# Layer 0's experts: two loads of weights wait also for the last store of layer 1's projected values

## The chip, the cores and the metric

The kernel runs on one core of one Trainium2 chip. The metric is the device time of one launch in microseconds; a kernel's time is the median of its runs. All data are 32-bit floats.

## The reference, cut to what matters

Four layers work on `x` (2 x 512 tokens of width 256). Each layer is a cross-attention against a context `ctx_1024` (2 x 1024 rows of width 256), followed by a feed-forward part with eight experts. The change lies in layer 0's experts, where work for layer 1's attention is done as well. Cut from the reference:

```python
x = x + _L0_xattn_ref(_layernorm(x), ctx_1024, ...)
x = x + _L0_ffn_ref(_layernorm(x), L0_ffn_router_w, L0_ffn_router_b, L0_ffn_w1, L0_ffn_w2)
x = x + _L1_xattn_ref(ctx_1024, _layernorm(x), ...)     # and so on to layer 3

def _L0_ffn_ref(...):            # 1024 tokens, 8 experts, hidden width 1024
    route = softmax(x @ router_w + router_b)
    max_prob, max_ind = max(route), argmax(route)
    for e in range(8):
        a, g = split(x @ w1[e], 2)
        y = silu(a) * g @ w2[e]
        out = where(max_ind == e, y, out)
    return out * max_prob

def _L1_xattn_ref(x, latents, ...):   # x is the context here
    xn = layer_norm(x, gamma_x, beta_x)
    kv_x = xn @ Wkv                   # keys and values: 512 columns each
    ...
```

Layer 1's keys and values of the context (`kv_x`) don't depend on layer 0, so the kernel can project them ahead of time.

## The kernel before

Layer 0's expert part begins with the router (normalise `X`, transpose, logits, softmax, the best expert of each token). `slots_of` gives each token a row ("slot") in the scratch tensor `xd` in DRAM. `moe` then does this, in the order of the code:

1. Eight indirect DMAs on POOL (L429) scatter the normalised tokens into `xd`; the list `put` holds them.
2. `filler()`, here `first_batch`: the context is transposed into `cT`, and `ahead1` projects layer 1's keys and values for the first of the two batches. These are sixteen jobs (eight of keys, eight of values): two `mm2` products into a PSUM tile `pk` (tags `a` and `g` in turn, two buffers each), a copy on ACT (ScalarE) into an SBUF tile of tag `sk` (two buffers; `sk` at L644 for keys, `sv` at L664 for values), and a store of 256 KB on ACT's queue to `kd` (L648) or `vd` (L665).
3. The experts' tiles. Expert weights are rows of `L0_experts`; one expert's tile `w` is 128 x 6144 floats (3072 KB), from a pool with four buffers. There are four pair tiles (`pair_tile`), which serve two experts with 64 slots each and so load two `w` (L475, on SP's queue), and six to eleven overflow tiles (`slot_tile`) of 128 slots for one expert, whose weights are gathered by an indirect DMA on POOL (L536). The loop runs pair 0, slot tile 4, pair 1, slot tile 5, and so on. Ahead of pairs 1 to 3 `between` puts two of the second batch's key jobs (`ahead1`).

Each tile loads its 128 slots from `xd` (`xs`, L455, on SP), transposes them on TensorE (PE, L464), copies them to `sT` on VectorE (L466) and runs the products. In a pair tile these are `half` (L489, into `pa` of tag `a` and `pg` of tag `g`, the same PSUM buffers that `pk` uses), the transposes `turn` (L503) and `product` (L510). In a slot tile they are `mm2` (L132) into `pa` and `pg`, and the second product (L561). The result goes to `yd` by ACT's queue.

The four `w` buffers go, in this order, to pair 0 (two), slot tile 4 and pair 1's first load; pair 1's second load takes a buffer of pair 0 when that is done, slot tile 5's load takes the other one, and so on. Pair 0's two loads are issued during the end of layer 0's attention (468.34 us).

`behind_slots(x)` makes a DMA `x` wait on a semaphore for the landing of `first_slots[0]`, the first tile's `xs` load. It is called for both loads of pairs 1 to 3, and for the slot tile 4's load (`if front < E and s == front`).

The order of instructions on each engine and queue is made by the framework from dependencies and readiness, not taken over from the code: on SP, the `xs` loads of four tiles stand ahead of pair 1's first weight load, though the code has them in turn. Each queue runs its instructions in order; one that waits holds up those behind it. The code pins an order only where it says so (`keep_in_program_order`, `pe_in_order`), which this stage does not. A `tc.If` after the last certain tile holds the rare overflow tiles, and after it comes the gather of the results (`combine`), on which layer 1 depends.

Of the kernel before, what the change touches and what calls it, by code (L numbers as in the profile page):

```python
# [33 lines left out]
def tile_kernel(ctx: ExitStack, tc: tile.TileContext, d: dict, out: bass.AP):  # L34
    nc = tc.nc
# [12 lines left out]
    def load_rows(pool, src, tag, bufs=None):  # L48

        rows, cols = src.shape  # L50
        return load(pool, [P, rows // P, cols], src.rearrange("(t p) f -> p t f", p=P), tag, bufs)

    def load_bc(pool, src, tag):

        n = src.shape[0]
        return load(pool, [P, n], src.partition_broadcast(P), tag)
# [48 lines left out]
    def to_T(*args, **kw):  # L105
        for _ in turn_blocks(*args, **kw):
            pass
# [21 lines left out]
    def mm2(ps_ap, lhsT, lcols, rhs, rcols):  # L129

        for dc in range(2):
            nc.tensor.matmul(  # L132
                ps_ap, lhsT[:, dc, lcols], rhs[:, dc, rcols], start=(dc == 0), stop=(dc == 1)
            )
# [110 lines left out]
    def bc8(a):  # L245
        return a[:, :, None].to_broadcast([P, TT, E])
# [4 lines left out]
    def router_logits(ps, srcT, w):  # L251
        pl = ps.tile([P, TT, E], F32, tag="mm", name="pl")
        for t in range(TT):
            mm2(pl[:, t, :], srcT, slice(t * P, (t + 1) * P), w, slice(0, E))
        lg = rt("lg")
        nc.vector.tensor_copy(lg, pl)
        return lg

    def maxed(src, name):
        m = rt(name, (TT,))  # L260
        nc.vector.tensor_reduce(m, src, AX.X, ALU.max)
        return m

    def summed(src, name):
        m = rt(name, (TT,))
        nc.vector.tensor_reduce(m, src, AX.X, ALU.add)
        return m
# [141 lines left out]
    def moe(L, ps, hp, ep, rows, slots, wrow, used, F, act, glu, finish, filler=None, hold=None, between=None):  # L409
# [13 lines left out]
        for i, si in enumerate(slots):  # L423
            if named and i == 0:
                nc.vector.tensor_copy(rows[:, :, D], c_tok)
            for t in range(TT):
                if i == 1:
                    nc.vector.tensor_scalar(rows[:, t, D:], c_tok[:, t : t + 1], float(NT), None, ALU.add)
                x = nc.gpsimd.indirect_dma_start(  # L429
                    out=xd, out_offset=bass.IndirectOffsetOnAxis(ap=si[:, t : t + 1], axis=0), in_=rows[:, t, :], in_offset=None  # L430
                ).ins
                for y in put:
                    tc.declare_no_dep(x, y, reason="rows of different slots")
                put.append(x)
        if filler is not None:
            filler()
        wd = d[f"{L}_experts"]
        WC = wd.shape[1]

        first_slots = []  # L440

        def behind_slots(x):

            tc.add_manual_dep(
                x, first_slots[0].name, mybir.DependencyInfo(mybir.DependencyClass.Sync, mybir.DependencyReason.DATA),
                reason="not among the transfers that the first tile waits for",
            )

        def parts(w):
            w1 = w[:, 0 : 2 * W1].rearrange("p (c f) -> p c f", c=2)  # L450
# [183 lines left out]
    def ahead(ps, st, L, w, src, jobs, values, bias=None, n_bias=1):  # L634


        for i, job in enumerate(jobs):
            pk = ps.tile([P, 512], F32, tag="ag"[i % 2], name="pk")
            if job[0] == "k":
                _, row, col, cols, c0 = job  # L640
                mm2(pk, w, cols, src, slice(c0, c0 + 512))
                k = st.tile([P, 512], F32, tag="sk", name="sk", bufs=2)
                if bias is None:
                    nc.scalar.copy(k, pk)  # L644
                else:
                    j = row // P % n_bias
                    nc.scalar.activation(k, pk, AF.Identity, bias=bias[:, j : j + 1])
                nc.scalar.dma_start(kds[L][row : row + P, col : col + 512], k)  # L648
            else:
                values(pk, job[1])  # L650

    kds, vds = {}, {}

    def ahead1(ps, st, w, cT, b, part=slice(None)):

        if b == 0:
            kds["L1"] = dram.tile([B * 4 * P, S], F32, tag="L1kd", name="kd")
            vds["L1"] = dram.tile([B * S, 512], F32, tag="L1vd", name="vd")

        def values(pv, kt):  # L660
            r = slice(b * S + kt * P, b * S + (kt + 1) * P)
            mm2(pv, cT, r, w, slice(512, 1024))
            v = st.tile([P, 512], F32, tag="sk", name="sv", bufs=2)
            nc.scalar.copy(v, pv)  # L664
            nc.scalar.dma_start(vds["L1"][r, :], v)  # L665

        jobs = []
        for pr in range(4):
            for hf in range(2):
                jobs.append(("k", (b * 4 + pr) * P, hf * 512, slice(pr * P, (pr + 1) * P), b * S + hf * 512))  # L670
        jobs += [("v", kt) for kt in range(8)]
        ahead(ps, st, "L1", w, cT, jobs[part], values)

    def ahead16(ps, st, L, params, nkt):

        one17, wk, wv, bk, bv = params[1:4] + params[5:7]
        NK = nkt * P
        kds[L] = dram.tile([B * 4 * P, NK], F32, tag=f"{L}kd", name="kd")
        vds[L] = dram.tile([B * NK, 512], F32, tag=f"{L}vd", name="vd")
        vs = [st.tile([P, 2, 16, 32], F32, tag=f"sv{i}", name="sv", bufs=1) for i in range(2)]  # L680
        for v in vs:
            nc.gpsimd.memset(v, 1.0)

        def values(pv, n):
            b, k2 = divmod(n, nkt // 2)
            v = vs[n % 2]
            for i in range(2):
                c0 = b * S + (k2 * 2 + i) * P
                mm2(pv[:, i * D : (i + 1) * D], cTr, slice(c0, c0 + P), wv, slice(0, D))
            from_ps = pv.rearrange("p (i h c) -> p i h c", i=2, c=16)  # L690
            if bv is None:
                nc.scalar.copy(v[:, :, :, 0:16], from_ps)
            else:
                for i in range(2):
                    nc.vector.tensor_add(v[:, i, :, 0:16], from_ps[:, i], bv.rearrange("p (h c) -> p h c", c=16))
            r0 = b * NK + k2 * 2 * P
            nc.scalar.dma_start(
                vds[L][r0 : r0 + 2 * P, :].rearrange("(i p) f -> p i f", p=P), v.rearrange("p i h c -> p i (h c)")
            )

        jobs = []
        for b in range(B):
            for g in range(4):
                for hf in range(NK // 512):
                    jobs.append(("k", (b * 4 + g) * P, hf * 512, slice(g * P, (g + 1) * P), b * S + hf * 512))
        jobs += [("v", n) for n in range(B * nkt // 2)]
        bias, cols = (one17, 1) if bk is None else (bk, 4)
        ahead(ps, st, L, wk, cTr, jobs, values, bias, cols)
# [51 lines left out]
    def psum(tags, name):  # L760

        return tc.tile_pool(name=name, bufs=tags, space=PSUM, reuse_waits="tile")

    def normed(pool, twice, tag="xn", width=D):
        xn = pool.tile([P, TT, width], F32, tag=tag, name="xn")
        layernorm(xn[:, :, 0:D], X, TT, twice)
        return xn
# [3 lines left out]
    with (  # L771
# [39 lines left out]
        cT = cp.tile([P, 2, B * S], F32, tag="cT", name="cT")  # L811
# [215 lines left out]
    wkv = load_rows(pp, d["L1_xattn_Wkv"], "wkv")  # L1027
# [4 lines left out]
    with (  # L1032
        tc.tile_pool(name="L0f", bufs=1, reuse_waits="tile") as fp,
        tc.tile_pool(name="L0h", bufs=2, reuse_waits="tile") as hp,
        tc.tile_pool(name="L0g", bufs=4, reuse_waits="tile") as ep,
        psum(2, "L0fps") as ps,
    ):
        rw = load_rows(fp, d["L0_ffn_router_w"], "rw")
        rb = load_bc(fp, d["L0_ffn_router_b"], "rb")
        xT = fp.tile([P, 2, B * S], F32, tag="cT", name="xT")  # L1040
        xn = normed(fp, False)
        to_T(ps, xT, xn, TT)
        lg = router_logits(ps, xT, rw)
        nc.vector.tensor_add(lg, lg, rb[:, None, :].to_broadcast([P, TT, E]))
        nc.vector.tensor_sub(lg, lg, bc8(maxed(lg, "m1")))
        nc.scalar.activation(lg, lg, AF.Exp)
        tot = summed(lg, "m2")
        nc.vector.reciprocal(tot, tot)
        nc.vector.tensor_mul(lg, lg, bc8(tot))
        mp = maxed(lg, "m1")  # L1050
        oh = first_of(lg, mp, "oh1")
        slots, wrow, used = slots_of(ps, [oh], 11, 64)
        cT = fp.tile([P, 2, B * S], F32, tag="cT", name="cT")

        def first_batch():
            to_T(ps, cT, C, CT, g_c, b_c, "g")
            ahead1(ps, hp, wkv, cT, 0)

        def between(s):

            if s > 0:
                ahead1(ps, hp, wkv, cT, 1, slice(2 * s - 2, 2 * s))

        yd = moe("L0", ps, hp, ep, xn, slots, wrow, used, 1024, AF.Silu, True, plain, first_batch, None, between)
        ahead1(ps, hp, wkv, cT, 1, slice(6, None))
        combine(fp.tile([P, TT, D], F32, tag="xn", name="yg"), yd, slots, [mp], X)

# [521 lines left out]
    first = {}  # L1589
# [268 lines left out]
```

## Time and profile before

| | before |
|---|---|
| time, median of 3 runs (lowest to highest) | 2259.86 us (2259.75 to 2261.13) |
| the profiled execution's own time | 2264.73 us |
| span of its trace | 2262.7 us |
| mean granted clock of PE | 0.95 |
| PE busy | 2070.5 us (92%) |
| VectorE (DVE), ACT, POOL busy | 1083.6, 859.6, 439.3 us |
| layer 0's experts: first weights issued, first pair product, gather of results | 468.34, 529.03, 667.18 us |

A profiled execution is about 5 us longer than the median here, of which 2 us lie around the span. Times inside the trace count from the start of the span. In rows of the trace, `pa<-w,sT` reads "the tile `pa` is written from `w` and `sT`", `x8` counts records, and a float32 product of two matrices shows as two records. A bracket at the end of a timeline row gives the idle time of the engine ahead of it and what ended that.

### The profile page before, as it was taken

The page shows a single profiled execution, that of the slowest core. Times are in us where ns is not written, and L with a number is a line of the kernel's source. Part 1 is how long each engine was busy: PE and PEld are TensorE (multiplying, and loading weights), DVE is VectorE, ACT ScalarE, POOL GpSimd, SP SyncE. Part 2 cuts the span into 40 slices and gives each one's busy share as a digit, 9 for nine tenths or more (in the row PEclk, how much of TensorE's full clock was granted, in tenths as well). Part 3 has the DMA queues.
Part 4 walks back from the last instruction along what each step waited for, and adds up shares of the span by engine and source line. Part 5 has one row for each costly group of instructions (what it writes and reads, how often), then busy time and mean ns, then how long its engine had stood idle before and what let it go on. Part 6 is the DMA issues. An engine that isn't in the chain of part 4 may idle for free. (4 is left out here: it accounts for less than half of the span.)

```text
span 2262.7 us, 29983 instructions
## 1 busy us (share of the span) xinstructions
PE 2070.5 (92%) x11532; PEld 1218.9 (54%) x11532; DVE 1083.6 (48%) x2157; ACT 859.6 (38%) x1645; POOL 439.3 (19%) x420
## 2 busy tenths in 40 slices
PE   7999999987998999999998998899699999579996
PEld 3444444353674444545586344599433333479995
DVE  7666666740125656655213884110377773322223
ACT  4444444421115565555112333222135556223333
POOL 2222223210012112111101122322123310111110
PEclk9999999988998999999899998999789999689998
DMA  4222222257945011001464512688310101547872
GB/s 129 71 62 75 71 75 58 87 208 298 372 146 121 29 34 39 21 11 65 142 231 146 202 35 79 221 310 312 104 47 30 34 15 25 248 180 297 321 303 64
DMA packets 111703, 300.72 MB, mean 133 GB/s; under 512 B 23232, under 2 KB 76224, under 8 KB 102848
## 3 DMA queue, kind: packets, MB, share of 16 engines
q1 hardware_dynamic: 76048, 159.30, 21.1%
q0 software_dynamic: 9888, 104.49, 11.9%
q10 hardware_dynamic: 25616, 34.90, 4.2%
q8 instruction: 97, 1.59, 0.3%
q14 instruction: 54, 0.44, 0.1%
HBM read 242.93 MB, written 47.66 MB: 128 GB/s over the span
## 5 line engine op out<-in xcount | busy, mean ns | idle before, releaser
L1452 ACT ACTIVATE p<-s 128x512 f32<-128x512 f32 (+3 forms) x384 | 185.9, 545 | 176.3 <-PE s L1451 114.8
L1394 PE MATMUL s<-kT,qT 32*128 32x512 f32 (+3 forms) x768 | 217.4, 612 | 8.7 <-DVE nm L1400 4.6
L132 PE MATMUL pa<-sT,w 128*128 128x128 f32 x1664 | 204.7, 278 | 8.0 <-DVE sT L466 3.7
L132 PEld LDWEIGHTS pa<-sT,w 128*128 128x128 f32 x1664 | 197.0, 193 | 16.4 <-ACT sq L1633 5.8
L561 PE MATMUL y<-w,hT 128*128 128x256 f32 x832 | 194.1, 386 | 7.2 <-ACT hT L551 3.3
L1451 PE MATMUL s<-qA,kT 32*128 32x512 f32 (+3 forms) x768 | 196.4, 587 | 1.2 <-ACT p L1452 0.9
L1404 DVE TENSOR_REDUCE mx<-s 128x1 f32<-128x512 f32 x256 | 163.6, 685 | 56.1 <-PE s L1394 35.5
L561 PEld LDWEIGHTS y<-w,hT 128*128 128x128 f32 x832 | 155.7, 193 | 30.0 <-DVE hT L558 5.2
L1139 ACT ACTIVATE p<-s,nm 128x512 f32<-128x512 f32 x192 | 129.5, 686 | 83.8 <-DVE nm L1136 83.8
L969 ACT ACTIVATE p<-s 128x1024 f32<-128x1024 f32 x128 | 124.1, 1021 | 89.9 <-PE s L964 89.9
L970 DVE TENSOR_SCALAR p<-p 128x1024 f32<-128x1024 f32 x128 | 107.3, 846 | 95.9 <-ACT p L969 95.7
L1136 DVE TENSOR_REDUCE nm<-s 128x2 f32<-128x1024 f32 x96 | 113.2, 1221 | 83.1 <-PE s L1132 83.1
L149 POOL TENSOR_TENSOR kT<-kT,turned 128x512 f32<-128x512 f32 x62 | 100.6, 1629 | 215.3 <-DVE turned L147 209.2
L975 DVE TENSOR_TENSOR acc<-acc,p 128x1024 f32<-128x1024 f32 x96 | 132.6, 1381 | 2.8
L895 PE MATMUL o<-p,v 128*64 128x512 f32 x512 | 125.9, 609 | 3.8 <-DVE p L970 3.8
L132 PE MATMUL pg<-sT,w 128*128 128x128 f32 x1056 | 129.0, 275 | 0.0
L964 PE MATMUL s<-qT,kT 64*128 64x512 f32 x512 | 127.2, 615 | 0.0
L558 DVE TENSOR_TENSOR hT<-act,pg 128x512 f32<-128x512 f32 x66 | 45.2, 688 | 167.9 <-PE pg L132 148.8
L132 PEld LDWEIGHTS pg<-sT,w 128*128 128x128 f32 x1056 | 123.6, 192 | 0.0
L148 POOL TENSOR_TENSOR kT<-kT,cos 128x512 f32<-128x512 f32 x62 | 87.9, 1427 | 134.7 <-DMA turned<-kT 61.2
L1427 PE MATMUL o<-p,v 128*32 128x256 f32 (+3 forms) x1280 | 106.6, 404 | 6.7 <-POOL p L1456 6.5
L1153 PEld LDWEIGHTS pt<-ident,p 128*128 128x128 f32 x768 | 85.9, 141 | 49.8 <-issue 24.7
(295 smaller groups left out, 3054.3 us busy)
## 6 DMA issues: line engine op xcount, KB each, us to landing
w<-in_L_experts_dram SPq DMA_DIRECT2D x8, 3200.0 KB
w<-in_L_experts_dram SPq DMA_DIRECT2D x8, 3072.0 KB
w<-in_L_experts_dram SPq DMA_DIRECT2D x8, 2048.0 KB
w<-in_L_experts_dram SPq DMA_DIRECT2D x8, 1536.0 KB
kd<-sk ACTq DMA_DIRECT2D x40, 256.0 KB
kT<-kd SPq DMA_DIRECT2D x16, 512.0 KB
turned<-kT SPq DMA_DIRECT2D x60, 128.0 KB
v<-vd SPq DMA_DIRECT2D x12, 512.0 KB
```

What stands on the lines that cost most here:

```text
L132: nc.tensor.matmul(ps_ap, lhsT[:, dc, lcols], rhs[:, dc, rcols], start=(dc == 0), stop=(dc == 1))
L561: nc.tensor.matmul(y, hT[:, f, :], w2[:, f, :], start=(f == 0), stop=(f == FT - 1))
L895: nc.tensor.matmul(G[n]["o"][64 * j : 64 * j + 64, :], V[g, b][:, kt, pr * P + 64 * j : pr * P + 64 * j + 64], p[:, j, :], start=(kt == 0) ...
L964: nc.tensor.matmul(s1[:, j, :], G[n]["kT"][r, kt * P : (kt + 1) * P], G[n]["qT"][r, :], start=True, stop=True)
L969: G[n]["exp"] = nc.scalar.activation(p, s1, AF.Exp, scale=0.125).ins
L975: nc.vector.tensor_add(G[n]["acc"], G[n]["acc"], p)
L1136: nc.vector.tensor_reduce(nm[:, qt, :, c], s1, AX.X, ALU.max, negate=True)
L1139: nc.scalar.activation(p[:, j, :], s1[:, j, :], AF.Exp, bias=nm[:, qt, j, c : c + 1], accum_out=l[:, qt, j, c : c + 1],)
L1394: nc.tensor.matmul(s1[:, :w], qT[r, qt * P : (qt + 1) * P], kT[r, c * 512 : c * 512 + w], start=True, stop=True)
L1404: nc.vector.tensor_reduce(mx[:, qt, j, c : c + 1], s1, AX.X, ALU.max)
L1451: nc.tensor.matmul(s2[:, qs], kT[r, kt * P : (kt + 1) * P], qA[r, qs], start=True, stop=True)
L1452: nc.scalar.activation(p[:, j, qs], s2[:, qs], AF.Exp, scale=0.25)
```

## The change

`ahead1` now collects the instruction of each store of projected values in a list `stored` and returns it; `first_batch` hands it on, and `moe` keeps what `filler()` returns. `behind_slots` adds a second semaphore wait to the same loads: beside `first_slots[0]` they wait for `stored[-1]`, the eighth and last store of values of the first batch, to land. Only layer 0 has such loads; the fillers of other layers return nothing, and nothing there reads it.

```diff
@@ -432,8 +432,7 @@
                 for y in put:
                     tc.declare_no_dep(x, y, reason="rows of different slots")
                 put.append(x)
-        if filler is not None:
-            filler()
+        stored = filler() if filler is not None else None
         wd = d[f"{L}_experts"]
         WC = wd.shape[1]
 
@@ -441,10 +440,12 @@
 
         def behind_slots(x):
 
-            tc.add_manual_dep(
-                x, first_slots[0].name, mybir.DependencyInfo(mybir.DependencyClass.Sync, mybir.DependencyReason.DATA),
-                reason="not among the transfers that the first tile waits for",
-            )
+
+            for y in (first_slots[0], stored[-1]):
+                tc.add_manual_dep(
+                    x, y.name, mybir.DependencyInfo(mybir.DependencyClass.Sync, mybir.DependencyReason.DATA),
+                    reason="not among the transfers that the first tile waits for",
+                )
 
         def parts(w):
             w1 = w[:, 0 : 2 * W1].rearrange("p (c f) -> p c f", c=2)
@@ -657,12 +658,14 @@
             kds["L1"] = dram.tile([B * 4 * P, S], F32, tag="L1kd", name="kd")
             vds["L1"] = dram.tile([B * S, 512], F32, tag="L1vd", name="vd")
 
+        stored = []
+
         def values(pv, kt):
             r = slice(b * S + kt * P, b * S + (kt + 1) * P)
             mm2(pv, cT, r, w, slice(512, 1024))
             v = st.tile([P, 512], F32, tag="sk", name="sv", bufs=2)
             nc.scalar.copy(v, pv)
-            nc.scalar.dma_start(vds["L1"][r, :], v)
+            stored.append(nc.scalar.dma_start(vds["L1"][r, :], v).ins)
 
         jobs = []
         for pr in range(4):
@@ -670,6 +673,7 @@
                 jobs.append(("k", (b * 4 + pr) * P, hf * 512, slice(pr * P, (pr + 1) * P), b * S + hf * 512))
         jobs += [("v", kt) for kt in range(8)]
         ahead(ps, st, "L1", w, cT, jobs[part], values)
+        return stored
 
     def ahead16(ps, st, L, params, nkt):
 
@@ -1054,7 +1058,7 @@
 
         def first_batch():
             to_T(ps, cT, C, CT, g_c, b_c, "g")
-            ahead1(ps, hp, wkv, cT, 0)
+            return ahead1(ps, hp, wkv, cT, 0)
 
         def between(s):
```

## The prediction, made before the result was known

> **What bounds the kernel now.** The page first: TensorE (PE) is busy 92% of the span, so time is won only where PE stands still or runs at a low clock. The chain of waits that ended last names no piece before 1665 us, so the stage of the change (layer 0's experts) is read from its own views: the waits between 440 and 560 us, then the timelines of PE, ACT, SP and POOL there, then two-microsecond windows with the granted clock. The longest waits of that stretch that end at PE's door:
>
> ```profile
> ACT sv L664 <- DMA vd<-sv: 22.6, 5, 16.1
> PE pa L489 <- ACT sv L664: 12.1, 1, 12.1
> POOL w L536 <- DMA vd<-sv: 5.9, 1, 5.9
> ```
>
> PE's first product of the first pair tile waits 12.1 us for a copy by ACT, and that copy waits 16.1 us for a store of projected values to land. The timelines (start, length, line, in brackets the idle time before and who ended it) show why:
>
> ```profile
> 511.09 0.33 SPq L475 DMA_DIRECT2D w<-in_L_experts_dram  x1
> 511.98 0.98 POOL L536 DMA_INDIRECT w<-in_L_experts_dram,wrow  x1 [5.92 <-DMA vd<-sv]
> ...
> 511.09 0.36 ACTq L665 DMA_DIRECT2D vd<-sv  x1
> 512.36 0.33 ACTq L665 DMA_DIRECT2D vd<-sv  x1
> 528.40 0.59 ACT L664 COPY sv<-pk 128x512 f32<-128x512 f32 x1 [16.07 <-DMA vd<-sv]
> 535.40 0.33 ACTq L665 DMA_DIRECT2D vd<-sv  x1
> ...
> 682.81 0.33 ACTq L665 DMA_DIRECT2D vd<-sv  x1
> 684.90 0.59 ACT L664 COPY sv<-pk 128x512 f32<-128x512 f32 x1 [0.86 <-DMA vd<-sv]
> ```
>
> Stores 3 and 4 of eight leave at 511.09 and 512.36, together with two weight loads of 3.15 MB each. Store 3 frees its buffer only at 528.40, 17.3 us later. With no weights in flight (682.81 to 684.90) the same 256 KB store needs 2.1 us. PE's side:
>
> ```profile
> 502.79 13.90 PE L132 MATMUL pk<-wkv,cT 128*128 128x512 f32 x32
> 516.52 0.38 PE L464 MATMUL pt<-ident,xs 128*128 128x128 f32 x2
> 529.03 3.68 PE L489 MATMUL pa<-w,sT 128*64 128x512 f32 x8 [12.13 <-ACT sv L664]
> 545.98 2.05 PE L132 MATMUL pa<-sT,w 128*128 128x128 f32 x16
> ...
> 561.06 2.34 PE L489 MATMUL pa<-w,sT 128*64 128x512 f32 x7 [0.56 <-ACT sk L644]
> 574.69 2.05 PE L132 MATMUL pa<-sT,w 128*128 128x128 f32 x16
> 589.77 1.94 PE L489 MATMUL pa<-w,sT 128*64 128x512 f32 x8 [0.56 <-ACT sk L644]
> 602.58 2.05 PE L132 MATMUL pa<-sT,w 128*128 128x128 f32 x16
> ```
>
> Each L489 row opens a pair tile and the next L132 `pa` row the slot tile behind it: pair 0 lasts 545.98 - 529.03 = 16.95 us, pair 1 13.63, pair 2 12.81. The clock explains part of pair 0's excess:
>
> ```profile
> 520.00:522.00 2.00, 0.00 (x0) 0.00 (x0) 0.00 (x0) 0.00 (x0) 0.00 (x0) 0.72 1.01 434
> 532.00:534.00 2.00, 1.99 (x6) 0.53 (x6) 0.00 (x0) 1.17 (x2) 0.00 (x0) 0.50 0.23 88
> 534.00:536.00 2.00, 2.00 (x10) 0.59 (x8) 0.00 (x0) 0.77 (x2) 0.00 (x0) 0.87 0.47 175
> ```
>
> The three last columns are granted clock, DMA share and GB/s. The clock falls to 0.50 about 4 us after PE stops and is back about 5.5 us after it restarts.
>
> **The change part by part.** Two weight loads now leave only after store 8 has landed: the slot tile 4's load on POOL (L536) and pair 1's first load on SP (L475). The same wait is also written on the other loads of pairs 1 to 3, which wait for buffers until 546 us or later and so pay nothing.
>
> *Gain 1, the stores.* Without weights beside them, stores 3 and 4 land 2.1 us after 511.09 and 512.36. Copies 5 to 8 (0.59 us each, one pair of buffers) then follow at about 513.2, 514.5, 515.9 and 517.2, the last one bounded by PE, whose last `pk` ends at 516.7. Store 8 leaves at 517.8 and lands at 519.9 (519.5 to 521.5 by the 2.1 to 2.9 us that such stores took before the weights came). Pair 0 no longer waits for a copy: PE's transposes end at 516.9, VectorE's copy of 0.42 us follows, and the first `pa` starts at 517.4 in place of 529.03: 11.6 us.
>
> *Gain 2, pair 0 warm.* PE has run without a gap up to there, so pair 0 takes 12.9 us (pair 2's 12.81) instead of 16.95: 4.1 us. It ends at 530.3, 15.7 us earlier than 545.98.
>
> *Loss 1, the moved loads.* Behind the waiting SP load stand two small `xs` loads for tiles transposed at 588 us and later, and pair 1's second weight load, which cannot leave before pair 0 ends: nobody pays. Behind the POOL load stands only slot tile 5's load, which waits for the same end. The price is the slot tile 4's weights themselves. POOL needed 0.9 us from its release (511.05) to the issue, so the issue is at 520.8. The row for its landing:
>
> ```profile
> DMA to landing us min/median/max: 19.1/19.1/19.1
> ```
>
> That load shared the queues with pair 1's load and with 0.5 MB of stores that will now be gone; 0.5 MB at the 0.43 MB per us of those windows is 1.2 us, so I take 18.0 us: landing at 538.8. The same POOL load took 17.0 to 20.6 us later in the stage; two loads of 6.3 MB at 0.43 need 14.6 us plus about 1.8 for the ends, so 16.4 to 20.6 are the bounds. PE, ready at 530.3, waits 8.5 us. This wait is what is late next.
>
> *Loss 2, the clock.* A wait of 8.5 us is longer than the 4 us after which the clock fell, so slot tile 4 starts at half clock. Over 5.5 us that loses 2.75; a slot tile that started cold at 1994.71 us took 3.77 us for its first sixteen products, against 1.79 warm, and 0.24 more for the next: 2.2. I take 2.5. [...]
>
> *Gain 3, pair 1.* Its second load, issued at 546.07, was late: pair 1 took 0.8 us more than pair 2, and PE stood 0.5 us for it. Now it leaves at 530.3, behind the two held loads; 12.6 MB from 520.8 at 0.43 end near 551, and pair 1 begins at about 556. 0.8 us back.
>
> Sum: 11.6 + 4.1 - 8.5 - 2.5 + 0.8 = 5.5 us. From slot tile 5 on each load leaves at the same distance from the tile that frees its buffer, so the rest of the stage keeps its shape, and the later layers start from its result: the shift reaches the end. The profiled execution took 2264.73 us (span 2262.7) and would take 2259.2; the runs' median, 2259.86, becomes 2254.4. Ends: store 8 at 519.5, a load of 16.4 and a clock loss of 2.0 give a wait of 6.5 and a gain of 8.0; 521.5, 20.6, 2.75 and no Gain 3 give 0.3.
>
> **The rivals.**
>
> *Slot tile 4's load gets the queues alone.* If pair 1's first load comes to stand behind the second small `xs` load on SP, whose buffer is freed only during pair 0 (about 528), the POOL load goes alone. Alone, such a load's median over the whole kernel is 11.0 us: landing at 531.8, a wait of 1.5, no cold clock. Then DMA paces pair 1 (four loads end near 553, used at 562.8 before): a gain of about 9.5, 2250.4. For it: SP's order isn't that of the code, since four `xs` loads stand ahead of the weight load. Against: that order follows what is ready, and store 8 lands before 528. 0.12.
>
> *The weights are the bound.* If the stage went at the pace of its weights, every us of held loads (511.1 to 520.0: 8.9) would come out at the end: 2268.8. It decides if loading starts late and never has a pause; for it, the DMA share is 0.9 to 1.0 over most of 550 to 640. Against: the share is 0 from 538 to 544, 0.09 after 640, and only pairs 1 and 3 wait for weights, 0.5 us each. [...] 0.10.
>
> *The last store is late.* ACT takes it after pair 0's activation (with its table load of 1.28 us): it would land near 524, the load at 543, and the gain shrinks to about 1.4: 2258.5. Against: pair 0's second `pg` needs the buffer that copy 8 frees. 0.08.
>
> *Nothing is held*, because the store has landed anyway: 2259.9. The store left at 535.40, so no. Below 0.01.
>
> **How the numbers follow.** The main case has 0.70, with its own range 2251.9 to 2259.6. A measurement of this kernel can tell about 0.2%, 4.5 us, from no change. The main case's 5.5 lies just beyond: I give 0.49 of it to a gain over 4.5 and 0.21 to one below. Faster: 0.49 + 0.12 = 0.61; slower 0.10; same the rest, 0.29. The range leaves out the slow rival and the edges: 2249.5 to 2259.5.
>
> **What would show it.** In the changed profile ACT's longest wait for `vd<-sv` is under 4 us, pair 0's `pa` (L489) starts near 517, the POOL load near 521, and slot tile 4's first `pa` near 539 with clock 0.50 in the windows ahead of it and about 4 us into it; `pk` after it starts near 552 instead of 556.68. A slot tile 4 that starts at 545 or later, a pair 1 over 13.6 us, or a gap in the `pk` stream before 517 would make the prediction wrong.

## The result and the profile after

The changed kernel took 2248.79 us (median of 9 runs) beside 2259.75 us for the kernel before (9 runs): ratio 0.9958, 95% interval 0.9941 to 0.9975, so about 9.5 us less (5.6 to 13.3). The two medians alone differ by 11.0 us; from here on the ratio with its interval counts. Two more comparisons, with the experiments, gave 0.9958 (0.9937 to 0.9980) and 0.9975 (0.9959 to 0.9992). 5.5 us had been predicted. The profiled execution took 2243.8 us, with a span of 2241.7.

The start of layer 0's expert stage moves by some us from one execution to the next, so from here on places are counted from the first scatter on POOL (`xd<-xn`): 495.98 us before, 489.91 after. Timeline of ACT, SP and POOL in the changed kernel (start, length, line; in brackets the idle time ahead):

```profile
507.54 0.58 ACT L667 COPY sv<-pk 128x512 f32<-128x512 f32 x1 [2.12 <-DMA vd<-sv]
...
511.31 0.58 ACT L667 COPY sv<-pk 128x512 f32<-128x512 f32 x1 [0.48 <-DMA vd<-sv]
511.92 0.33 ACTq L668 DMA_DIRECT2D vd<-sv  x1
...
514.53 0.33 SPq L476 DMA_DIRECT2D w<-in_L_experts_dram  x1
...
515.53 0.98 POOL L537 DMA_INDIRECT w<-in_L_experts_dram,wrow  x1 [15.56 <-ACT act L497]
```

Copy 5 (the fifth copy of values) waited 2.12 us where it had waited 16.07, and store 8 left at 511.92 where it had left at 535.40. The two weight loads follow it. POOL's bracket names `act`, but POOL follows SP by 1.0 us here as it did before (0.9): both were released by store 8's landing. (In the kernel that holds the loads to store 6, POOL's load leaves 2.5 us before that `act`.) TensorE:

```profile
511.40 1.94 PE L490 MATMUL pa<-w,sT 128*64 128x512 f32 x8 [0.56 <-ACT sv L667]
...
524.20 0.44 PE L465 MATMUL pt<-ident,xs 128*128 128x128 f32 x2
532.14 3.42 PE L132 MATMUL pa<-sT,w 128*128 128x128 f32 x16 [7.50 <-DMA w<-in_L_experts_dram,wrow]
535.39 1.95 PE L132 MATMUL pg<-sT,w 128*128 128x128 f32 x16
...
547.73 2.26 PE L490 MATMUL pa<-w,sT 128*64 128x512 f32 x8
...
560.86 2.05 PE L132 MATMUL pa<-sT,w 128*128 128x128 f32 x16
```

Pair 0 starts 0.56 us after PE is ready (before: 12.13 us) and ends at 524.20, 12.80 us after its start. Then PE waits 7.50 us for slot tile 4's weights, and its first sixteen products take 3.42 us where warm ones take 2.05.

The stage in all the kernels of this study, in us after the first scatter, up to the gather that ends it:

| kernel | pair 0 starts | slot tile 4 starts | slot tile 5 starts | gather | ratio to before (95%) |
|---|---|---|---|---|---|
| before | 33.06 | 50.00 | 78.72 | 171.20 | 1 |
| after, three profiles | 21.49 to 21.50 | 42.23, 42.80, 42.54 | 70.95, 72.63, 72.33 | 163.61, 165.54, 164.71 | 0.9958, 0.9958, 0.9975 (above) |
| only POOL's load held | 21.49 | 49.89 | 79.41 | 172.37 | 1.0003 (0.9985 to 1.0021) |
| only SP's load held | 21.50 | 41.56 | 70.17 | 163.09 | 0.9967 (0.9949 to 0.9986) |
| spare buffers | 21.49 | 43.90 | 72.68 | 165.63 | 0.9979 (0.9961 to 0.9998) |
| pair 1's load in four | 21.49 | 48.56 | 76.91 | 169.27 | 0.9990 (0.9975 to 1.0005) |
| held to store 6 | 21.48 | 40.75 | 70.61 | 163.55 | 0.9975 (0.9959 to 0.9991) |
| spare buffers, POOL's queue, twice | 21.49, 21.50 | 35.53, 35.29 | 64.86, 66.22 | 157.97, 159.50 | 0.9948 (0.9927 to 0.9968), 0.9952 (0.9931 to 0.9972) |
| spare buffers, two wide stores | 21.49 | 35.58 | 66.24 | 158.76 | 0.9951 (0.9929 to 0.9972) |

Where slot tile 5 starts decides where the gather comes, to within about 1 us (92.4 to 93.3 us lie between in every row). And the stage agrees with the time: 171.20 less the gather column, over 2260 us, lies inside every interval of the last column. The change's stage became 5.7 to 7.6 us shorter, mean 6.6. The kernel before has one profile, so the 171.20 has no spread of its own; the changed kernel's stage spreads over 1.9 us. The two profiled executions differ by 20.9 us (2264.73 against 2243.8), but 6 us of that lie ahead of the stage, where the change edits nothing, and 7 behind it; the changed kernel's three profiled spans (2241.7, 2245.6 and 2253.1) show how far its executions differ.

### The profile page after: what moved, and what is told of

Read it like the earlier page. It is cut to its first block, busy times and chain, and to the rows that moved or that the text cites. A ratio compares the mean times of both kernels' runs of the same rounds, so it can differ in the third digit from the quotient of the medians.

```text
span 2241.7 us, 29984 instructions
## 1 busy us (share of the span) xinstructions
PE 2051.5 (92%) x11532; PEld 1209.8 (54%) x11532; DVE 1083.0 (48%) x2157; ACT 858.9 (38%) x1645; POOL 437.6 (20%) x420
## 5 line engine op out<-in xcount | busy, mean ns | idle before, releaser
L1157 PEld LDWEIGHTS pt<-ident,p 128*128 128x128 f32 x768 | 86.4, 142 | 50.0 <-issue 24.6
```

## The experiments

The theory: two weight loads stretch stores 3 and 4 (17.2 and 19.7 us from issue to landing before) and with them pair 0; held back, they cost slot tile 4 its weights, one for one. The rivals: the order and the clock set the stage and not that load; or the weights' total pace does.

**The change again, beside the first three.**

> The changed kernel again, beside the three that take it apart. The measure is the stage: from the first scatter of slots on POOL to the first gather of results there, 171.2 us in the profile of before and 163.6 in the first profile of after. Theory (queues in turn): the two weight loads take turns row by row with the stores, the stores take 17 us, ACT has two buffers and so PE waits; holding both loads removes that. It expects 163 to 164 again, pair 0 about 21.5 us after the first scatter, and a time 5 to 13 us below before. Rival (order and clock): the gain came from the changed order of PE and SP (one pair of transposes drawn ahead) and from a favourable clock ahead of the stage; then this stage would spread between 164 and 171.

The time came as expected, about 9.5 us less. The stage did not: 165.54 (second value in each cell) is above the 163 to 164 of the theory and inside the 164 to 171 of the rival. Most of the 1.9 us beyond the first profile is a clock that came back later (in the part on the prediction below); the next two experiments decide against the rival.

**Only POOL's load held (slot tile 4's).** In the changed kernel SP's loads lose the new wait (the two comments are added here):

```diff
-        def behind_slots(x):
+        def behind_slots(x, store):
-            for y in (first_slots[0], stored[-1]):
+            for y in (first_slots[0], stored[-1]) if store else (first_slots[0],):
...
-                    behind_slots(x)          # pair_tile, SP
+                    behind_slots(x, False)
-                    behind_slots(x)          # slot_tile, POOL
+                    behind_slots(x, True)
```

> Only slot tile 4's load on POOL waits for the last store; pair 1's first load on SP leaves as in before. Queues in turn: one weight load beside the stores instead of two halves the turns, a store takes about 9 us instead of 17; pair 0 starts about 25 us after the first scatter (33.1 before, 21.5 after), the last store lands near 31, the POOL load near 46, and the stage lasts about 167 us, 4 less than before and 3 to 4 more than after. Order and clock: PE's and SP's order is that of the changed kernel, so the stage lasts 164 like there.

Nothing was won: 1.0003. SP's, POOL's and PE's timelines:

```profile
505.43 9.22 SPq L456 DMA_DIRECT2D xs<-xd  x5
514.70 0.43 SPq L476 DMA_DIRECT2D w<-in_L_experts_dram  x1
...
526.53 0.98 POOL L537 DMA_INDIRECT w<-in_L_experts_dram,wrow  x1 [23.09 <-issue]
...
543.27 3.75 PE L132 MATMUL pa<-sT,w 128*128 128x128 f32 x16 [15.16 <-DMA w<-in_L_experts_dram,wrow]
```

SP's load got out at 21.32, later than expected (the fifth `xs` load, which waits for pair 0's buffer, now stands ahead of it; the five are issued from 505.43 to 514.65, the weight load at 514.70), and only store 8 (21.91) met it. That one store took some 10 us, and POOL's load waited for it: issued at 33.16 in place of 25.6, and landed 16.6 us later. Pair 0 was as early as in the changed kernel (21.49), yet slot tile 4 was where it had been before (49.89), and so was the time. So what counts is when slot tile 4's weights land, not when pair 0 starts. The forecast of 167 missed by over 5 us: the store landed about 1 us later than the 31 expected, the load landed at 49.8 and not near 46, and the first sixteen products after the wait of 15.16 us took 3.75 us, a cold start.

**Only SP's load held (pair 1's first).** The edit is the same with `True` and `False` exchanged.

> Only pair 1's first load on SP waits for the last store; slot tile 4's load on POOL leaves as in before. Queues in turn: pair 0 starts near 25 us after the first scatter, slot tile 4's weights land before pair 0 is done (near 28), so slot tile 4 starts near 38 without a wait and with a warm clock; then pair 1's weights are late by some 2 us. Stage about 161 to 162, so better than the full change by about 2. Order and clock: PE's order is that of before, so the stage lasts 171.

Stage 163.09, slot tile 4 at 41.56: as good as the change. POOL's load left at 15.66 and landed 12.43 us later, long before it was needed. Both are later than expected (161 to 162, and 38), because one load beside it was enough to hold store 4 (issued at 505.50) for 12 us:

```profile
517.45 0.58 ACT L667 COPY sv<-pk 128x512 f32<-128x512 f32 x1 [9.40 <-DMA vd<-sv]
...
518.09 3.50 PE L490 MATMUL pg<-w,sT 128*64 128x512 f32 x8 [4.88 <-ACT sv L667]
...
531.34 2.05 PE L132 MATMUL pa<-sT,w 128*128 128x128 f32 x16
```

Here pair 0 paid inside (4.88 us and a cold start), and slot tile 4 did not wait at all. The price was shifted, not avoided. These two kernels also put the rival of order and clock out: it expected a stage of 164 where PE's order is that of the changed kernel (POOL's load held, 172.37) and of 171 where it is that of before (here, 163.09).

**Spare buffers, nothing held.** To the kernel before: the last four values are staged in `xn` (the scatter's source, free once that has landed), so that copies 5 to 8 need no store to land.

```diff
+            if spare is not None and kt >= 4:
+                v = spare[:, 2 * kt - 8 : 2 * kt - 6, :].rearrange("p a f -> p (a f)")
+            else:
-            v = st.tile([P, 512], F32, tag="sk", name="sv", bufs=2)
+                v = st.tile([P, 512], F32, tag="sk", name="sv", bufs=2)
...
-            ahead1(ps, hp, wkv, cT, 0)
+            ahead1(ps, hp, wkv, cT, 0, spare=xn)
```

> The kernel before, nothing held, but the last four stores of projected values are made from the normalised tokens' tile, which is free by then, so that no copy by ACT waits for a store to land. Every engine's order is that of before. Queues in turn: the stores are as slow as in before, but nobody waits for them: pair 0 starts at 21.5 us after the first scatter, slot tile 4's weights land near 35, as in before, when pair 0 is done, so its wait is 0 to 2 us; pair 1's second load leaves at 34.5 and lands near 51. Stage about 156 to 158 us, a time 13 to 15 us below before. Order and clock: 171.

Pair 0 started at 21.49 as expected, the stage took 165.63 and not 156 to 158. ACT's timeline:

```profile
512.22 0.59 ACT L667 COPY xn<-pk 128x512 f32<-128x512 f32 x1 [0.96 <-PE pk L132]
523.07 0.33 ACTq L668 DMA_DIRECT2D vd<-xn  x1
523.48 1.28 ACT L496 ACT_TABLE_LOAD   x1 [10.67 <-DMA w<-in_L_experts_dram]
```

ACT had copied the value and then stood over 10 us at the issue of store 8 (the bracket of 10.67 us counts the issue in), until SP's *weight load* had landed, although the store neither reads nor writes anything of it. The semaphores that the trace keeps with each instruction say why. In the kernel before, the transfers on SP's and ACT's queues complete on eight semaphores (101 to 105 and 107 to 109, each 86 to 88 times), and stores 5 to 8, which complete on 109, 101, 102 and 104, each have ahead of them on ACT's queue a wait for that same semaphore (528.4 to 534.8 us). Here SP's weight load completes on 104, and so does store 8; its issue waits for 104, whose last update comes at 522.99. It was not ACT's own queue that came free: store 3, its oldest store in flight, landed at 523.17, after the issue. Pair 0 stood for it (its `turn` waited 7.81 us).

**Pair 1's load in four.** Why does a 256 KB store take 17 us? In the DMA view of the kernel before, 519 to 525 us (queue: packets, MB, share; q10 is ACT's, q1 SP's, q0 POOL's):

```profile
q0 software_dynamic: 55, 1.35, 52.3%
q1 hardware_dynamic: 49, 1.20, 46.6%
q10 hardware_dynamic: 52, 0.11, 4.5%
```

The three queues move nearly the same number of packets, and by their sizes (1.35 MB in 55, 0.11 MB in 52) a packet is a row: 24.6 KB of weights, 2 KB of a store. (From 518.6 to 520.5 us the same view has exactly 16 of each, as many as there are DMA engines.) That gives an estimate from these numbers, if the engines take the queues in turn and the rows are spread evenly: a store has 128 rows, 8 on each of 16 DMA engines; a turn through the three queues moves 51 KB at 27 KB per us and engine (0.43 MB per us over 16), 1.9 us. Eight turns are 15 us, and with the 2.1 us of a store by itself 17, as measured for store 3 (17.2); store 4, which left 1.3 us later, took 19.7. A load has 128 rows too, so store 3 landed together with SP's load that left with it (528.32 and 528.13): the landing alone can't tell turns from a wait for the load's end, the packets can. To test the turns, rows of 6 KB on SP's queue, in the kernel before:

```diff
-                x = nc.sync.dma_start(w, wd[(2 * s + j) * P : (2 * s + j + 1) * P, :]).ins
-                if s > 0:
-                    behind_slots(x)
+                for c in range(0, WC, WC // 4) if s == 1 and j == 0 else (0,):
+                    cs = slice(c, c + WC // 4) if s == 1 and j == 0 else slice(0, WC)
+                    x = nc.sync.dma_start(w[:, cs], wd[(2 * s + j) * P : (2 * s + j + 1) * P, cs]).ins
+                    if s > 0:
+                        behind_slots(x)
```

> The kernel before (no wait added); pair 1's first weight load is cut into four transfers of a quarter of the columns, so its rows are 6 KB instead of 24 KB, same bytes. Question: why does a 256 KB store take 17 us beside two weight loads. If the queues take turns row by row (a turn beside two loads moves 24.6 + 24.6 + 2 KB), a turn is now 24.6 + 6.1 + 2 KB and the store of 128 rows needs about 10 us: copy 5 of the projected values starts some 7 us earlier than before, pair 0 starts at about 26 us after the scatter instead of 33.1. If a queue gets its share by its bytes or the store waits for the load to end, it stays at about 17 us and pair 0 at 33. Open: the four transfers also take four completion semaphores, and a later store may inherit one of them; then the store that inherits stands until its quarter has landed. Time: gain of up to 5 us by the first, none by the second.

Store 4 left at 507.04, and copy 6, which needs its buffer, came 15 us later:

```profile
522.11 0.58 ACT L666 COPY sv<-pk 128x512 f32<-128x512 f32 x1 [14.06 <-DMA vd<-sv]
```

So neither 10 nor 17. The DMA view of the two stretches 508 to 512 us and 512 to 518 us:

```profile
q1 hardware_dynamic: 152, 0.84, 52.2%
q0 software_dynamic: 30, 0.74, 45.8%
q10 hardware_dynamic: 13, 0.03, 1.7%
```

```profile
q0 software_dynamic: 80, 1.97, 76.4%
q1 hardware_dynamic: 85, 0.42, 17.7%
q10 hardware_dynamic: 81, 0.17, 7.1%
```

In the second stretch the queues move equal numbers of packets again (80, 85, 81), and SP's queue gets about a fifth of the bytes that POOL's gets for the same turns. In the first, ACT's queue gets 13 beside 152 and 30. Turns by row fit the second stretch; the slow start of store 4 stays open. Pair 0 started at 21.49, since store 3 left 0.9 us ahead of the loads and landed in 3.8 us; it then stood 10.17 us inside for copy 6. The time (0.9990) can't be told from before.

**Held to store 6.** The change with `stored[5]` in place of `stored[-1]`.

> The change, but the loads wait for the sixth of the eight stores instead of the last. Theory (slot tile 4's weights pace the stage one for one): both loads leave about 2.7 us earlier; the last two stores then run beside them and land late, but nobody waits for their buffers before pair 0's second half; slot tile 4 starts at 39.5 to 40.5 instead of 42.2 to 42.8, the stage lasts 161 to 162, about 2.5 us under the changed kernel. Rival (any store beside the loads costs PE): the second half of pair 0 waits 5 us or more for copy 8 or its buffer, and nothing is won.

```profile
513.07 0.98 POOL L537 DMA_INDIRECT w<-in_L_experts_dram,wrow  x1 [12.81 <-ACT sv L667]
...
530.95 3.75 PE L132 MATMUL pa<-sT,w 128*128 128x128 f32 x16 [6.40 <-DMA w<-in_L_experts_dram,wrow]
```

POOL's load left at 22.87 (2.75 us earlier) and landed in 17.75 us instead of 16.6, with store 8 beside it; slot tile 4 started at 40.75, 1.5 to 2 us earlier than in the changed kernel. Nobody waited for the last two stores, so the rival (pair 0 pays for any store beside the loads) is out. The direction is as expected, the size short: 39.5 to 40.5 and a stage of 161 to 162 were expected, and the stage (163.55) is that of the changed kernel's best profile. In the time (0.9975) it can't be told from the change either.

**Spare buffers, stores on POOL's queue.** To the spare buffers, which hold nothing back, one edit more:

```diff
-            nc.scalar.dma_start(vds["L1"][r, :], v)
+            issue = nc.gpsimd if spare is not None and kt >= 4 else nc.scalar
+            issue.dma_start(vds["L1"][r, :], v)
```

> The kernel before, nothing held; the last four values are staged in a spare buffer (free at that time) and their four stores leave on POOL's queue, behind slot tile 4's weight load, instead of ACT's. So neither the buffers nor ACT can stop PE. Theory (the path is the weights of slot tile 4, and everything ahead of them that waits for stores can be taken off it): pair 0 starts at 21.5 us after the scatter and ends at 34.4, slot tile 4's load leaves at 16 and lands at 34 to 35, so slot tile 4 starts at 34.5 to 36 at full clock, slot tile 5 at 63 to 65, the stage lasts 157 to 159, 13 us less than before and 7 less than the changed kernel: time about 0.6% below before. Rival (order and clock set the stage, not this load): stage about 163 to 165 as in the changed kernel. Rival (another hidden wait, such as a semaphore shared with a load): slot tile 4 again at 42 or later.

```profile
516.97 1.94 PE L489 MATMUL pa<-w,sT 128*64 128x512 f32 x8 [0.56 <-ACT xn L667]
...
531.01 2.02 PE L132 MATMUL pa<-sT,w 128*128 128x128 f32 x16 [1.17 <-DMA w<-in_L_experts_dram,wrow]
```

Pair 0 starts early *and* slot tile 4's weights, issued at 15.39, land 20.01 us later, 1.2 us after PE is ready. The clock stays up (2.02 us for the first sixteen). Slot tile 4 starts at 35.53 and the stage takes 157.97, all as the theory said. The four stores take 18 to 23 us each, and nobody waits. What is late next is pair 1's second load, issued when pair 0 is done: PE waits 0.44 us for it here and 2.04 in the second profile.

**Two wide stores.** The same buffers, the last four values in two stores of 512 KB on ACT's queue:

```diff
-            nc.scalar.dma_start(vds["L1"][r, :], v)
+            if spare is None or kt < 4:
+                nc.scalar.dma_start(vds["L1"][r, :], v)
+            elif kt % 2:
+                two = vds["L1"][r.start - P : r.stop, :].rearrange("(a p) f -> p a f", p=P)
+                nc.scalar.dma_start(two, spare[:, 2 * kt - 10 : 2 * kt - 6, :].rearrange("p (a c) f -> p a (c f)", a=2))
```

> The kernel before, nothing held; the last four values are staged in the spare buffer and leave on ACT's queue as two stores of 512 KB instead of four of 256 KB. With the spare buffer and four stores ACT stood 10.7 us at the issue of the last store until pair 1's weight load had landed. Theory (eight completion semaphores are dealt out in turn to the transfers of SP's and ACT's queues, and the last store had drawn the one that the weight load was still using): two stores fewer shift the turn, the last store draws the semaphore of a small transfer that has long landed, ACT does not stand, pair 0 starts at 21.5 us after the scatter and runs through, slot tile 4 starts at 34.5 to 36.5, the stage lasts 157.5 to 159.5, as in the kernel with POOL's queue. Rival (ACT's queue is full, or a store's issue waits while weights hold the queues): ACT stands again for about 10 us, slot tile 4 starts near 44 and the stage lasts about 165.

```profile
512.98 0.38 ACTq L672 DMA_DIRECT2D vd<-xn  x1
515.12 1.28 ACT L496 ACT_TABLE_LOAD   x1 [2.17 <-PE pa L489]
```

The 10.67 us are gone, with the same bytes on the same queue beside the same loads; the two wide stores complete on 109 and 102, semaphores of `xs` loads that had landed, and slot tile 4 starts at 35.58. With the trace of the four stores this shows that the shared semaphore, and not a full queue, had held ACT.

**Both again, side by side.**

> The kernel with the spare buffer and the last four stores on POOL's queue, a second time, for its ratio beside the changed kernel on the same chip. By the length of the stage (158.0 against 163.6 to 165.5 us) it should be 5.6 to 7.5 us faster than the changed kernel: ratio to before 0.994. If something later in the kernel gives it back, it is no faster than the changed kernel.

> The changed kernel, a second time, beside the two others: ratio to before 0.995 to 0.997; stage 163.5 to 166 us; slot tile 4 at 42 to 43 us after the scatter.

On the same chip: 2246.61 us with POOL's queue, 2247.89 with the two wide stores, 2251.67 for the change. A ratio of 0.994 had been expected for POOL's queue, and 0.995 to 0.997 for the change (0.9975 came). With either way of sending the last stores, the stage with spare buffers is 4 to 8 us shorter than the changed kernel's in every profile; the ratios (0.9948, 0.9952 and 0.9951 against 0.9958, 0.9958 and 0.9975) lean the same way, but their intervals overlap. Against the kernel before the gain is clear, about 11 us; against the change it is shown by the traces only.

## Why the prediction was right, step by step

| step, us after the scatter | predicted | after, three profiles |
|---|---|---|
| pair 0 starts (*Gain 1*) | 21.4 | 21.49 to 21.50 |
| pair 0 lasts (*Gain 2*) | 12.9 | 12.80 in the first |
| POOL's issue (*Loss 1*) | 24.8 | 25.62, 25.91, 25.52 |
| slot tile 4 starts (*Loss 1*) | 42.8 | 42.23, 42.80, 42.54 |
| cold clock (*Loss 2*) | 2.5 | 1.45, 2.89, 2.84 |
| pair 1 lasts (*Gain 3*) | 12.8 | 13.13, 12.80, 12.81 |

*Gain 1* and *Gain 2* came as worked out: without weights beside them, copies waited 0.45 to 2.12 us for stores (first profile). That they alone are worth nothing is shown by the kernel with POOL's load held: early pair 0, no gain.

*Loss 1* had two errors that nearly cancel, which is luck. POOL's issue was 0.7 to 1.1 us late: in the first profile store 8's landing and the release took 3.6 us and not the 3.0 allowed (511.92 to 515.53), in the other two store 8 itself left later (22.89 and 22.49 in place of 21.8). And the landing took 16.6 to 17.0 us in place of 18.0, near the lower bound of 16.4. The 1.8 us that this bound has for the ends of a load were the author's estimate; in the trace of before, the semaphores of stores 5 to 8 have their first update 1.82 to 1.84 us after the issue. The estimate took 1.2 us off the 19.1 for the missing stores; 2.1 to 2.5 came off.

*Loss 2* was of the right size on the average, but it is no fixed number: its bounds, 2.0 to 2.75, leave out all three profiles. It is read from where pair 1 starts: before, 15.08 us lie between the start of slot tile 4 and that of pair 1; of these 0.94 are pair 1's transposes, which the changed program runs in the wait (the row at 524.20). The rest, 14.14, became 15.59, 17.03 and 16.98. Two-microsecond windows say why (granted clock, DMA share and GB/s last), first in the first profile, then in the third (the last line is PE's restart there):

```profile
526.00:528.00 2.00, 0.00 (x0) 0.00 (x0) 0.00 (x0) 0.00 (x0) 0.00 (x0) 1.00 0.92 393
528.00:530.00 2.00, 0.00 (x0) 0.00 (x0) 0.00 (x0) 0.00 (x0) 0.00 (x0) 0.56 0.98 416
...
532.00:534.00 2.00, 1.86 (x9) 1.89 (x10) 0.00 (x0) 0.00 (x0) 0.00 (x0) 0.50 1.00 426
534.00:536.00 2.00, 2.00 (x15) 2.00 (x15) 0.00 (x0) 0.41 (x1) 0.00 (x0) 0.74 1.02 433
536.00:538.00 2.00, 2.00 (x21) 2.00 (x20) 0.55 (x1) 0.19 (x1) 0.00 (x0) 1.00 1.06 455
```

```profile
538.00:540.00 2.00, 2.00 (x11) 2.00 (x11) 0.00 (x0) 0.15 (x1) 0.00 (x0) 0.50 0.96 409
540.00:542.00 2.00, 2.00 (x12) 2.00 (x11) 0.00 (x0) 0.45 (x1) 0.00 (x0) 0.53 1.00 430
542.00:544.00 2.00, 2.00 (x20) 2.00 (x20) 0.69 (x1) 0.00 (x0) 0.00 (x0) 1.00 0.99 414
...
536.06 3.75 PE L132 MATMUL pa<-sT,w 128*128 128x128 f32 x16 [7.81 <-DMA w<-in_L_experts_dram,wrow]
```

PE restarts at 532.14 and has its clock back at about 535.0 (a clock of 0.74 is half speed for 1.04 of 2 us): 2.9 us. In the other profile it restarts at 536.06 and has it at 541.9: 5.8 us. Half of each delay is about the loss measured, 1.45 and 2.84 us. The prediction's upper bound rests on one measured delay, 5.5 us in the kernel before; the changed kernel shows about that length in one execution and half of it in another, and no run shows why.

*Gain 3* came (13.63 became 12.80 to 13.13), though pair 1's second load landed later than worked out: 0.3 us after pair 1 had started in the first profile and about 1.4 us before it in the others, where 5 us had been forecast.

The saving that was not foreseen is the 0.94 us: the order of instructions on PE changed, and two transposes of pair 1 went ahead of slot tile 4. On SP the fifth `xs` load went ahead of the weight load; there it cost nothing.

The rivals. *The weights are the bound* is out: from the start of pair 2 to the gather 77.40 us before and 77.58 after, and the kernel with spare buffers and POOL's queue, which holds no load back, needs 78.02. *Slot tile 4's load gets the queues alone* did not come: SP's load left 1 us ahead of it. *The last store is late* did not come: the table load stands behind store 8 (513.42 against 511.92).

The forecast was a gain of 5.5 us; the three ratios give 9.5, 9.5 and 5.6 us, with ends about 4 us to each side, and the stage's mean is 6.6. So the stage was 1 us better than forecast, by the 0.94 us of the transposes in the main and by the landing; what the first two ratios show beyond that (some 3 us) is within the intervals, and no run assigns it.

## What to carry to other kernels

Look at what is issued beside a small store that must land before a buffer is free: here two loads of 3.15 MB stretched one of 256 KB from 2.1 us to 17.2. While the queues moved equal numbers of packets (55, 49 and 52), its length fitted an estimate from its rows on each DMA engine (8) and one turn of all queues (1.9 us); with smaller rows on one queue that estimate fell short (15 us where about 10 had been worked out). Holding the loads moved the price to the tile that needs them first, so price that tile's wait (7.5 to 8.1 us here) and its cold restart (1.45 to 2.89 us); giving the stores a buffer of their own, so that nobody waits for them, took the price away (slot tile 4 at 35.3 to 35.6 in place of 42.2 to 42.8). When a wait for a buffer has been removed, read the issue of the next transfer: here it stood over 10 us for a weight load with which it only shared a semaphore.

## What the runs showed of the hardware that was not expected

- A 256 KB store took 2.1 us without weights in flight (kernel before), 10 to 12 us beside one load of 3.15 MB (the two kernels that hold one load), 15 us beside one such load and one cut into four (pair 1's load in four), and 17 to 20 us beside two (kernel before).
- A store's issue stood over 10 us for the landing of an unrelated weight load that completes on the same semaphore, 104 (spare buffers); with two wide stores in place of the last four, on 109 and 102, the 10.67 us were gone.
- After waits of 7.50 and 7.81 us TensorE's clock came back 2.9 us after the restart in one execution and 5.8 us in another of the changed kernel.
